# Graph attention with a residual and layer norm: when the residual of the last 26 tiles is gathered

## The chip, the cores and the metric

The kernel runs on one core of a Trainium2 chip. The metric is the device time of one execution in microseconds (us), median over several executions.

## The reference

For each of 16 graphs of 1024 nodes with 512 features: q, k and v are three projections of `x`; each node attends, in 8 heads of 64, to the nodes that its row of the 0/1 matrix `adj` names (one matrix for all graphs); the result is projected, added to `x`, and normalised.

```python
q, k, v = ((x @ W + b).reshape(B, N, 8, 64) for W, b in ((Wq, bq), (Wk, bk), (Wv, bv)))
scores = einsum('bqhd,bkhd->bhqk', q, k) / sqrt(64) + (1 - adj) * -1e9
out = einsum('bhqk,bkhd->bqhd', softmax(scores), v).reshape(B, N, 512)
x = layernorm(x + out @ Wo + bo)          # over the last axis, eps 1e-5, no affine
```

## The kernel before

`adj` is sparse, and the kernel never forms the dense scores. At the start it ranks the nodes by their number of neighbours, and from then on works on *tiles* of 128 nodes in that order: 8 tiles to a graph, 128 in all, numbered `b * 8 + t`. The list of original rows of tile `t` is the column `asked_row[:, t]`. For each tile, `edges(t)` builds the lists of neighbours (`key_row`, `query_row`).

The attention itself runs in *blocks*. One block takes 128 pairs of a query and one of its neighbours: `gather` fetches 128 rows of k and v together (`kvg`, 512 KB, from the scratch `kv_rows` in device memory) by an indirect DMA, and once per tile the 128 query rows (`qt`, 256 KB, from `q_rows`); VectorE multiplies q and k (`products`, L889) and sums by head (`scores`, L893); ScalarE takes the exponential (L903) and, mostly, weighs v with it (`weigh`, L913); VectorE or TensorE adds the blocks of a tile up. A graph has 35 blocks, the whole run 560.

The projections are the other half ("fronts"): for pairs of node tiles of a *later* graph, `x` is loaded (L548, three buffers), transposed by TensorE (`pxT`), copied out by ScalarE (`xT`, L559), multiplied with the weights (a seven-product scheme, `pair`), and written to `q_rows` (L615, tile `q`, two buffers) and `kv_rows` (L628, tile `kv`, five buffers). The last stage, `finish`, multiplies the attention's result with Wo (`po`), adds the residual (`y`, L790), normalises and scatters the rows out (L816).

The order on every engine is written out by one loop over a step number `n`. It runs from -34; blocks 0 to 559 are due at steps 0 to 559, so steps -34 to -1 are a lead-in with the ranking, the lists and the first graph's projections. In step `n` the loop issues `gather(n + 8)`, `products(n + 4)`, `exponentials(n + 3)`, `weigh(n + 2)` or `(n + 1)`, and then as many matmul units of the fronts as its estimate of the step's length allows. Steps are positions in the engines' instruction lists, not times: each engine goes through its own list in order and waits for others by semaphores alone. Indirect DMAs are issued from GpSimd (POOL), plain ones of this part of the program from SyncE (SP); both lists are in order too.

The residual `y` of a tile is the tile's rows of `x` in the ranked order. For tiles 0 to 101 it is gathered straight from `x` when it is needed (L752, from `load_y`). For the last 26 tiles (`SPILL[0]` = 102 and up) it is put in order ahead of time: `sort_residual(i)` gathers the rows of tile 102 + i into an SBUF tile `y_sorted` (POOL, L752) and, two steps on, SP writes it to a scratch `residual[i]` in device memory (L760). Near the end of the run, `load_y` reads it from there with a plain DMA (L769). `y_sorted` shares the six buffers of tag `y` with the `y` of `load_y`, so the gather of copy i waits for the write of copy i - 6.

Two copies go at the end of each step that `SORTED_AT` names:

```python
SORTED_AT = range(-16, -3)
...
if n in SORTED_AT:
    for i in range(2):
        sort_residual(2 * (n - SORTED_AT[0]) + i)
```

Of the kernel before, what the change touches and what calls it, by code (L numbers as in the profile page):

```python
# [35 lines left out]

SPILL = range(102, 112)

SORTED_AT = range(-16, -3)
AHEAD_LAST = 11  # L40

ROWS = 3
# [118 lines left out]
def kernel(  # L161
# [67 lines left out]
    with ExitStack() as main:  # L229
# [122 lines left out]
        def later(k, fn):  # L352
            plan.setdefault(now[0] + k, []).append(fn)
# [397 lines left out]
        def gather_x(y, b, t):  # L751
            nc.gpsimd.indirect_dma_start(  # L752
                out=y, out_offset=None, in_=x_rows,
                in_offset=bass.IndirectOffsetOnAxis(ap=asked_row[:, t:t + 1], axis=0), element_offset=b * N * D,
            )

        def sort_residual(i):
            y = work.tile([P, D], F32, tag="y", name=f"y_sorted_{i}", bufs=Y_BUFS)
            gather_x(y, *divmod(SPILL[0] + i, NT))
            later(2, lambda: nc.sync.dma_start(residual[i], y))  # L760
# [117 lines left out]
        def products(n):  # L878
            b, t, i = blocks[n]
            if t == 0 and i == 0:  # L880
                norms = small.tile([P, NPAIR], F32, tag="lone", name=f"lone_{b}", bufs=1)
                later_last(0, lambda q=QT[b, t]: squares(f"q_{b}", q, norms, lone))
                later(2, lambda: nc.vector.tensor_reduce(lone_norm[:, b:b + 1], norms, axis=AX.X, op=OP.max))
            if i < OWN[t]:
                q = QT[b, t] if i < OWN[t] - 1 else QT.pop((b, t))
            else:
                q = QG.pop(n)
            QK[n] = work.tile([P, D], F32, tag="qk", name=f"qk_{n}", bufs=2)
            nc.vector.tensor_tensor(QK[n], q, KG[n][:, 0:D], op=OP.mult)  # L889

        def scores(n):
            S[n] = small.tile([P, HEADS], F32, tag="s", name=f"s_{n}", bufs=4)
            nc.vector.tensor_reduce(S[n], QK.pop(n).rearrange("p (h d) -> p h d", d=HD), axis=AX.X, op=OP.add)  # L893

        def exponentials(n):

            b, t, i = blocks[n]
            if i == 0:
                PV[n] = work.tile([P, D + HEADS], F32, tag="pv0", name=f"pv_{n}", bufs=3)
            else:  # L900
                PV[n] = work.tile([P, D + HEADS], F32, tag="pv", name=f"pv_{n}", bufs=PV_BUFS)
            bias = absent[:, own[t] + i:own[t] + i + 1] if i < OWN[t] else 0.0
            nc.scalar.activation(PV[n][:, D:], S.pop(n), AF.Exp, bias=bias)  # L903

        def by_act(n):
            b, t, i = blocks[n]
            return 0 < i < OWN[t] or n % 2 == 0 or n < NB // 2

        def weigh(n):
            v, pv = KG.pop(n), PV[n]  # L910
            if by_act(n):
                for h in range(HEADS):
                    nc.scalar.activation(  # L913
                        pv[:, ts(h, HD)], v[:, ds(D + h * HD, HD)], AF.Copy, scale=pv[:, D + h:D + h + 1]
                    )
                return
            nc.vector.tensor_tensor(
                pv[:, 0:D].rearrange("p (h d) -> p h d", d=HD),
                v[:, D:].rearrange("p (h d) -> p h d", d=HD),
                pv[:, D:, None].to_broadcast([P, HEADS, HD]), op=OP.mult,  # L920
            )

        def add_own(n):
            b, t, i = blocks[n]
            pv = PV.pop(n)
            if i == 0:
                PV[b, t] = pv
            else:
                nc.vector.tensor_tensor(PV[b, t], PV[b, t], pv, op=OP.add)  # L929
# [120 lines left out]
        with tc.manual_schedule():  # L1050
# [12 lines left out]
            n = -LEAD_IN  # L1063
            while n < total or plan or rest or urgent or done or finishing or spilled or not guarded:
                now[0] = n
                if n < 0:
                    share = LISTS_SHARE if n > -16 else LEAD_SHARE if n > -LEAD_IN else TRANSPOSE * 1.5
                elif n >= SPILL[0] // NT * NB + NB:

                    share = sum(u[0] for u in fronts) / max(fronts_end - n, 1) + NS * SUM / NB if fronts else LAST_SHARE  # L1070
                elif n % NB == 0:

                    left = sum(u[0] for u in fronts)
                    ahead = EARLY + FIRST * (1 - max(0, n // NB - 1) / (SPILL[0] // NT))
                    goal = fronts_time - (n // NB + 2 + ahead / NB) * batch_time
                    share = (max(0.0, left - goal) + NT * NPAIR * PRODUCT + NS * SUM) / NB
                if 0 <= n + 3 < total:
                    exponentials(n + 3)
                if 0 <= n + 4 < total:
                    products(n + 4)  # L1080
                while gathered[0] < min(n + (AHEAD if fronts else AHEAD_LAST) + 1, total) and blocks[gathered[0]][0] in set_up:
                    gather(gathered[0])
                    gathered[0] += 1
                if 0 <= n + 1 < total and not by_act(n + 1):
                    weigh(n + 1)
                if 0 <= n < total and blocks[n][2] < OWN[blocks[n][1]]:
                    add_own(n)
                if 0 <= n + 4 < total:
                    scores(n + 4)
                if 1 <= n <= total and (n == total or blocks[n][2] == 0):  # L1090
                    normalise(*blocks[n - 1][:2])
                for fn in plan.pop(n, ()):
                    fn()
                if 0 <= n + 2 < total and by_act(n + 2):
                    weigh(n + 2)
                for fn in rest.pop(n, ()):
                    fn()
                credit += share
                if 0 <= n < total and blocks[n][2] >= OWN[blocks[n][1]]:
                    add_up(n)  # L1100
                    credit -= SUM
                for tile_done in done[:0 if fronts and len(done) < LAZY else 1 if fronts else 2] + coming:
                    if tile_done not in loaded and sum(b * NT + t not in SPILL for b, t in Y) < 5:
                        load_y(*tile_done)
                coming[:] = [t for t in coming if t not in loaded]
                if spilled and not fronts and n > last_reload + 2 and sum(b * NT + t in SPILL for b, t in Y) < 3:
                    reload(*spilled.pop(0), reloads)
                    reloads, last_reload = reloads + 1, n
                first_unit = True
                while credit > 0 or urgent:  # L1110
                    if urgent and not (first_unit and fronts):
                        urgent.pop(0)()
                        continue
                    if (
                        not finishing and len(done) > (LAZY if fronts else 0) and n > loaded.get(done[0], n) + 1
                        and n > last_finish + 1 and not total - 2 <= n < total
                    ):
                        finishing = finish(*done.pop(0))
                        last_finish = n
                    units = finishing or fronts  # L1120
                    if not units:
                        if urgent:
                            urgent.pop(0)()
                            continue
                        break
                    cost, fn, ready = units[0]
                    if ready and not ready():
                        if urgent:
                            urgent.pop(0)()
                            continue  # L1130
                        break
                    del units[0]
                    fn()
                    credit -= cost
                    first_unit = False
                credit = min(credit, share)
                preps += prep.pop(n, [])
                preps = [g for g in preps if next(g, True) is None]
                if n in SORTED_AT:
                    for i in range(2):  # L1140
                        sort_residual(2 * (n - SORTED_AT[0]) + i)
                n += 1

    word = nc.values_load(  # L1144
# [32 lines left out]
```

## Time and profile before

| | us |
|---|---|
| median of four executions | 1985.45 (1982.45 to 1996.21) |
| the profiled execution | 1986.11 |
| its span, first to last instruction | 1984.3 |
| TensorE (PE) busy in it | 1913.2 |
| VectorE (DVE) busy | 1780.9 |
| ScalarE (ACT) busy | 1566.8 |
| GpSimd (POOL) busy | 1294.3 |
| the 26 gathers of `y_sorted` are issued | from 75.3 to 145.0 |
| the 26 writes to `residual` are issued | from 80.3 to 151.8 |
| the 26 reads from `residual` are issued | from 1782.1 to 1950.7 |

All times in the trace count from the start of the span. "DMA share" in the tables by stretch is the mean busy share of the core's 16 DMA engines, and can come out a little over 1. A wait is written `waiting instruction <- what ended the wait`, with the total in us, the times it occurred and the longest; `issue` means that nothing the trace shows was waited for, `remote` that what ended it is not among the recorded instructions. Names such as SPq are the queue of instructions of an engine that issues DMAs.

### The profile page before, as it was taken

To read this page: it belongs to the slowest core of one execution; us is meant where nothing else is said; L and a number is where in the kernel's file an instruction comes from. 1 tells how busy PE (TensorE), PEld (TensorE's weight loads), DVE (VectorE), ACT (ScalarE), POOL (GpSimd) and SP (SyncE) were. 2 spreads that over 40 slices of the span, in tenths; PEclk is the share of its full clock that TensorE was granted. 3 is DMA by queue.
4 is the path that set the end of the run, shared out by engine and by line. 5 is a ranking of instruction groups with operands and counts; after the bars stand their busy time and mean duration, and the time that the engine had idled before them with its cause. 6 is when DMAs were issued, how large, how long until landed. Compare 5 with 4: busy or idle time off the path is not lost. (4 is left out here: it accounts for less than half of the span.)

```text
span 1984.3 us, 25833 instructions
## 1 busy us (share of the span) xinstructions
PE 1913.2 (96%) x5379; PEld 923.5 (47%) x5379; DVE 1780.9 (90%) x3745; ACT 1566.8 (79%) x6152; POOL 1294.3 (65%) x1224
## 2 busy tenths in 40 slices
PE   8988999999999999999999999999999999999896
PEld 4434454444545454454545445444444545444443
DVE  3789999989999999999998999999899999999785
ACT  4526878878797888879887887879888798988795
POOL 1563566756777675767667586766757676566784
PEclk9999999999999999999999999999999999999898
DMA  6797887978989788888889788888978889988984
GB/s 255 227 341 247 262 303 248 300 270 278 314 267 318 258 304 282 300 286 281 305 262 321 255 302 274 299 304 266 314 256 285 287 299 322 316 307 287 319 286 146
DMA packets 191140, 563.10 MB, mean 284 GB/s; under 512 B 31711, under 2 KB 31739, under 8 KB 190974
## 3 DMA queue, kind: packets, MB, share of 16 engines
q0 software_dynamic: 121632, 403.22, 62.2%
q1 hardware_dynamic: 66736, 153.16, 20.8%
q10 hardware_dynamic: 2606, 4.99, 0.7%
q14 instruction: 122, 1.00, 0.2%
q8 instruction: 44, 0.72, 0.1%
HBM read 442.25 MB, written 143.71 MB: 295 GB/s over the span
## 5 line engine op out<-in xcount | busy, mean ns | idle before, releaser
L868 POOL DMA_INDIRECT kvg<-kv_rows,key_row x560 | 632.1, 1129 | 434.2 <-ACT pv L903 114.0
L913 ACT ACTIVATE pv<-kvg,pv 128x64 f32<-128x64 f32 x3608 | 908.7, 339 | 0.1
L584 PE MATMUL pq<-wq,xT 128*128 128x512 f32 x1024 | 478.7, 597 | 3.9 <-issue 1.7
L584 PE MATMUL po<-wo,oT 128*128 128x512 f32 x944 | 437.0, 595 | 4.7 <-DVE y L790 1.9
L893 DVE TENSOR_REDUCE s<-qk 128x8 f32<-128x512 f32 x560 | 380.5, 680 | 6.1
L889 DVE TENSOR_TENSOR qk<-qt,kvg 128x512 f32<-128x512 f32 x464 | 317.0, 683 | 3.8 <-DMA kvg<-kv_rows,key_row 3.3
L584 PEld LDWEIGHTS pq<-wq,xT 128*128 128x128 f32 x1024 | 191.3, 191 | 222.8 <-issue 207.3
L584 PEld LDWEIGHTS po<-wo,oT 128*128 128x128 f32 x944 | 175.5, 191 | 206.0 <-issue 191.2
L698 PE MATMUL pp<-t,s 128*128 128x512 f32 x504 | 238.6, 596 | 9.4 <-DVE s L570 9.4
L698 PE MATMUL x<-b,xT 128*128 128x512 f32 x504 | 237.1, 593 | 0.0
L929 DVE TENSOR_TENSOR pv<-pv,pv 128x520 f32<-128x520 f32 x336 | 232.9, 693 | 0.0
L903 ACT ACTIVATE pv<-s,absent 128x8 f32<-128x8 f32 x464 | 135.8, 294 | 106.4 <-DVE s L893 65.9
L816 POOL DMA_INDIRECT out_dram<-y,asked_row x128 | 151.4, 1183 | 38.9 <-issue 26.3
L852 POOL DMA_INDIRECT qt<-q_rows,asked_row x128 | 139.8, 1092 | 36.7 <-issue 34.3
L594 ACT ACTIVATE sq_k<-kv 128x128 f32<-128x128 f32 x512 | 150.7, 300 | 9.7 <-DVE kv L721 8.7
L698 PEld LDWEIGHTS pp<-t,s 128*128 128x128 f32 x504 | 95.2, 191 | 119.1 <-issue 107.1
L698 PEld LDWEIGHTS x<-b,xT 128*128 128x128 f32 x504 | 94.7, 190 | 112.2 <-issue 108.8
L752 POOL DMA_INDIRECT y<-in_x_dram,asked_row x102 | 115.4, 1131 | 30.6 <-issue 29.8
L862 POOL DMA_INDIRECT qg<-q_rows,query_row x96 | 105.7, 1102 | 26.8 <-issue 25.1
L698 PE MATMUL z<-b,s 128*128 128x512 f32 x252 | 118.6, 593 | 1.4 <-issue 0.7
L698 PE MATMUL z<-t,s 128*128 128x512 f32 x252 | 118.6, 593 | 0.0
L698 PE MATMUL pp<-t,xT 128*128 128x512 f32 x252 | 118.4, 592 | 0.0
(193 smaller groups left out, 2614.3 us busy)
## 6 DMA issues: line engine op xcount, KB each, us to landing
kv_rows<-kv SPq DMA_DIRECT2D x128, 512.0 KB
x<-in_x_dram SPq DMA_DIRECT2D x128, 256.0 KB
q_rows<-q SPq DMA_DIRECT2D x128, 256.0 KB
kvg<-kv_rows,key_row POOLq DMA_INDIRECT x560
residual<-y_sorted SPq DMA_DIRECT2D x26, 256.0 KB
y<-residual SPq DMA_DIRECT2D x26, 256.0 KB
adj<-in_adj_dram POOLq DMA_DIRECT2D x8, 512.0 KB
spill<-oT SPq DMA_DIRECT2D x10, 256.0 KB
```

Of the source, the lines that this page charges most:

```text
L584: nc.tensor.matmul(p, lhs()[:, ts(c, P)], w[:, c, :], start=(c == 0), stop=(c == NPAIR - 1))
L594: nc.scalar.activation(sq, s[:, ts(h, P)], AF.Square, scale=scale, accum_out=sums[:, h:h + 1])
L698: nc.tensor.matmul(R[bank], l[:, ts(c, P)], right[:, c, :], start=(first and c == 0), stop=(c == 1), skip_group_check=True,)
L752: nc.gpsimd.indirect_dma_start(out=y, out_offset=None, in_=x_rows, in_offset=bass.IndirectOffsetOnAxis(ap=asked_row[:, t:t + 1], axis=0), ...
L816: nc.gpsimd.indirect_dma_start(out=out_rows[b, t], out_offset=bass.IndirectOffsetOnAxis(ap=asked_row[:, t:t + 1], axis=0), in_=y, in_offse ...
L852: nc.gpsimd.indirect_dma_start(out=QT[b, t], out_offset=None, in_=q_rows[b % ROWS], in_offset=bass.IndirectOffsetOnAxis(ap=asked_row[:, t: ...
L868: nc.gpsimd.indirect_dma_start(out=KG[n], out_offset=None, in_=kv_rows[b % ROWS], in_offset=bass.IndirectOffsetOnAxis(ap=key_row[:, g:g + ...
L889: nc.vector.tensor_tensor(QK[n], q, KG[n][:, 0:D], op=OP.mult)
L893: nc.vector.tensor_reduce(S[n], QK.pop(n).rearrange("p (h d) -> p h d", d=HD), axis=AX.X, op=OP.add)
L903: nc.scalar.activation(PV[n][:, D:], S.pop(n), AF.Exp, bias=bias)
L913: nc.scalar.activation(pv[:, ts(h, HD)], v[:, ds(D + h * HD, HD)], AF.Copy, scale=pv[:, D + h:D + h + 1])
L929: nc.vector.tensor_tensor(PV[b, t], PV[b, t], pv, op=OP.add)
```

## The change

The same 26 copies are made, in the same order, two to a step, in 13 steps as before. The first eight copies stay at steps -16 to -13. The other 18 move from steps -12 to -4 to steps -3 to 5. As the steps are no longer consecutive, the copy's number comes from the position in the list.

```diff
-SORTED_AT = range(-16, -3)
+SORTED_AT = (*range(-16, -12), *range(-3, 6))
...
                 if n in SORTED_AT:
                     for i in range(2):
-                        sort_residual(2 * (n - SORTED_AT[0]) + i)
+                        sort_residual(2 * SORTED_AT.index(n) + i)
```

On PE, DVE and ACT the instructions and their order are the same in both programs. On POOL the 18 gathers move behind the gathers of blocks 0 to 5, and stand two by two between those of blocks 5 to 14; the gather of the first `y` (graph 0, tile 0) follows them. On SP the 18 writes move among the later writes of `q` and `kv` and loads of `x`. The list of block gathers and residual copies on POOL, from the fifth neighbour list on (`codes` is a gather of `adj` rows in `edges`; `s8` stands for `y_sorted` number 8):

```
before: s8 s9 codes4 s10 .. s15 codes5 s16 s17 qt0 kvg0 qt1 kvg1 codes6 s18 s19 kvg2 s20 s21 qt2 kvg3
        s22 s23 kvg4 s24 s25 qt3 kvg5 kvg6 kvg7 qt4 kvg8 kvg9 kvg10 kvg11 qt5 kvg12 kvg13 kvg14 y0 kvg15
after:  codes4 codes5 qt0 kvg0 qt1 kvg1 codes6 kvg2 qt2 kvg3 kvg4 qt3 kvg5 s8 s9 kvg6 s10 s11 kvg7 s12 s13
        qt4 kvg8 s14 s15 kvg9 s16 s17 kvg10 s18 s19 kvg11 s20 s21 qt5 kvg12 s22 s23 kvg13 s24 s25 kvg14 y0 kvg15
```

## The prediction

> **What bounds the kernel now.** I read the shares of the engines first, then the busy time by stretches, then the waits and the order of time where the 18 copies leave and where they arrive. (The page's chain that ended last reaches back only 4 us from the end, so it says nothing here.)
>
> ```profile
> PE 1913.2 (96%) x5379; PEld 923.5 (47%) x5379; DVE 1780.9 (90%) x3745; ACT 1566.8 (79%) x6152; POOL 1294.3 (65%) x1224
> ```
>
> TensorE is busy for 96% of the span. What a change wins in the lead-in is kept only if it lets PE start its long, nearly full stretch earlier. In the next answer the columns are the length, the busy time of PE, weight loads, DVE, ACT and POOL, the granted clock, the DMA share and GB/s.
>
> ```profile
> 75.00:100.00 25.00, 25.00 (x65) 11.46 (x64) 19.66 (x56) 7.04 (x25) 13.99 (x14) 1.00 0.90 305
> 100.00:125.00 25.00, 19.71 (x50) 7.87 (x48) 23.65 (x69) 5.36 (x21) 11.75 (x12) 1.00 0.91 310
> 125.00:150.00 25.00, 21.23 (x57) 9.65 (x57) 18.01 (x47) 6.53 (x29) 19.30 (x19) 1.00 1.01 373
> 150.00:175.00 25.00, 18.27 (x56) 9.01 (x55) 23.32 (x57) 10.67 (x43) 4.80 (x5) 0.93 0.67 246
> 175.00:200.00 25.00, 24.86 (x77) 11.93 (x76) 24.31 (x57) 20.98 (x88) 9.31 (x10) 1.00 0.77 246
> ```
>
> Until 100 us PE is full. From 100 to 175 it is idle for 5.29 + 3.77 + 6.73 = 15.8 us while DVE is busy 23.65, 18.01 and 23.32 of each 25: the neighbour lists are DVE work, and this stretch is DVE's. It is also where the DMA engines are full, 0.91 and 1.01. From 175 on PE is full again. So the prize is at most those 15.8 us, and only the part that the DMA traffic causes. In the stretch 138 to 160:
>
> ```profile
> DVE kv L726 <- ACT sq_q L594: 5.5, 1, 5.5
> ...
> PE pp L698 <- DVE s L570: 4.0, 1, 4.0
> ...
> DVE est L491 <- remote: 1.4, 1, 1.4
> ```
>
> DVE loses 5.5 + 1.4 = 6.9 us. The program's list of waits says what L726 (writing `kv`) needs: TensorE's `z`, recorded as done at 142.7, ScalarE's squares of the tile that had the buffer, done at 134.2, and the write of that tile to `kv_rows`, which SP issued at 132.8. DVE went on at 148.7. The `sq_q` that the answer names is not in that list; it only happened to end then. The `kv` write is the one candidate that no record shows done by 143. But a load of `x` on SP that waits for the same write went out at 145.8, so the write can explain DVE's wait to there and not the last 2.9 us. L491 waits for one small matmul recorded at 142.5 and was released at 150.8 by something not recorded. Both fall where DMA is fullest: 411 GB/s at a share of 1.04 from 145 to 150, 412 GB/s from 150 to 155. PE pays afterwards, since `s` on DVE (L570) comes late:
>
> ```profile
> 151.25 1.88 PE L698 MATMUL x<-b,xT 128*128 128x512 f32 x4
> 153.12 1.31 PE L513 MATMUL pe<-kl,of 128*128 128x82 f32 x10
> 158.41 3.40 PE L698 MATMUL pp<-t,s 128*128 128x512 f32 x4 [3.97 <-DVE s L570]
> ...
> 165.51 1.88 PE L698 MATMUL x<-b,xT 128*128 128x512 f32 x4
> ```
>
> Four matmuls of the same form take 1.88 us at 165.5 and 3.40 us at 158.4, after the gap of 3.97 us.
>
> **What the Trainium skill says.** (1) "DMA: Bandwidth & Descriptors", section "Issuing engines are not separate DMA queues": transfers started from any engine run on the same 16 DMA engines and interleave. The trace agrees: between 146 and 150 POOL's queue takes 58.5% of them and SP's 45.3%. (2) The same page, "Anatomy of one DMA": DMA engines don't wait on semaphores, the issuing sequencer does. So a copy that waits for its buffer holds up all behind it on POOL; the trace has 2.1 us of it, at 117.6 below. (3) "TensorE: Matmul & The Clock Gate", Part 1: after an idle window of about 3.4 us the array runs at half clock. The granted clock is 0.79 from 155 to 160 and 1.00 before, which agrees.
>
> **The change, part by part.**
> *Size.* A copy reads 256 KB and writes 256 KB; 18 of them are 18 x 0.524 = 9.4 MB. At the 410 GB/s of the fullest stretch that is 23.0 us of all DMA engines.
>
> *Taken away, steps -12 to -4.* The stretch 100 to 150 moved 17.1 MB; without the copies (part of whose traffic runs on to 158) it is about half full. DVE's own work there stays: 94% busy from 95 to 142, so nothing is won before 142. After that, on DVE 6.9 us go; on PE the waits of 4.0, 0.7 and 0.5 us (the last two shown as "issue" for `z` and `pq` between 143 and 150) and 3.40 - 1.96 = 1.4 us of slow clock, 6.6 us. With both engines alike I take **6 us won**. Bounds: 0, if these stalls have another cause (the "remote" release is unexplained); 9, if the 2.8 us that PE waits at 172 go too. What is late next is DVE, without a gap.
>
> *Moved past on POOL.* 18 gathers with the 0.3 us between two, 1.25 us each: 22.5 us of POOL, 2.5 us ahead of each of the gathers kvg6 to kvg14. POOL stands idle for about 36 us between 151 and 205, mostly for `weigh` of the block whose buffer the gather takes. So issue time is covered. If it weren't, it would be 2.5 us a step.
>
> *Moved into, as bandwidth.* Before, the free DMA share from 155 to 195 in stretches of 5 us is 0.26, 0.23, 0.50, 0.67, 0.27, 0.30, 0.30, 0.25: 2.78 x 5 = 13.9 us. The other 9.1 of 23.0 us must go into 138 to 155, which is half empty once the old copies are gone (17 x 0.5 = 8.5). It fits with nothing to spare. The first six, s8 to s13, can start about 138: kvg1 was issued at 126.8, and seven gathers of 1.3 us lie between.
>
> *The buffers.* A copy takes the `y` buffer of the copy six earlier, once that is written. The two legs under full DMA:
>
> ```profile
> 117.64 0.94 POOL L752 DMA_INDIRECT y_sorted<-in_x_dram,asked_row  x1 [2.10 <-DMA residual<-y_sorted]
> ...
> 144.98 0.95 POOL L752 DMA_INDIRECT y_sorted<-in_x_dram,asked_row  x1 [0.30 <-issue]
> ...
> 160.34 0.98 POOL L868 DMA_INDIRECT kvg<-kv_rows,key_row  x1 [7.98 <-DVE est L482]
> ...
> 190.33 0.99 POOL L868 DMA_INDIRECT kvg<-kv_rows,key_row  x1 [2.28 <-ACT sums L535]
> 191.62 0.96 POOL L752 DMA_INDIRECT y<-in_x_dram,asked_row  x1 [0.30 <-issue]
> ```
>
> Gather 25 was issued at 145.0 and its write went out at 151.8, so a gather took at most 6.9 us. Copy 16, at 117.6, waited for write 10, issued at 108.2: 9.5 us for a write. Six copies can turn round in 16.4 us, 5.5 us for a step of two. The new steps are shorter, 3 to 7 us. Forward with everything 6 us earlier than before: write 8 stands on SP behind the `kv` writes at 160.0, now 154, so s14 can go at 154 + 9.5 = 163.5, s20 at 180, and y0, which takes the buffer of s20, at 196.3. Before it went at 191.6, which would be 185.6 now.
>
> *Who waits for that.*
>
> ```profile
> 187.94 0.68 DVE L889 TENSOR_TENSOR qk<-qt,kvg 128x512 f32<-128x512 f32 x1
> ...
> 205.85 0.68 DVE L889 TENSOR_TENSOR qk<-qt,kvg 128x512 f32<-128x512 f32 x1
> ...
> 207.65 0.68 DVE L790 TENSOR_TENSOR y<-po,y 128x512 f32<-128x512 f32 x1
> ```
>
> The ninth `products` (block 8) is at 187.94 and kvg8 was issued at 160.34: 27.6 us in hand. Block 14 has 205.85 - 190.33 = 15.5, y0 has 207.65 - 191.62 = 16.0. In the new order kvg12 goes behind s20 and s21 at about 182.5 and is used at 193 (199.2 before): 10.7 in hand, above 6.9. y0, issued at 196.3 and landed by 203.2, is used by DVE at 201.6: **1.6 us late**, in the in-order list of DVE. The smaller risk on SP is that `q`, `kv` and `x` transfers stand behind a residual write that waits for its gather; SP lost 18.1 us to that in all before, and two buffers of `q` some 20 us apart cover 5 us of it. I add 0.4 and take **2 us given back**; bounds 0 (the legs are maxima) and the slower case below. DVE gets no instruction more. The reads of `residual` from 1782 us on are as they were.
>
> Sum: 6 - 2 = 4 us less than the profiled 1986.1 us (span 1984.3, to 1980.3). That execution is 0.7 us above the median of 1985.45, which is nothing here; the forecast median is 1981.5 us. About 0.5% (9.9 us) is what a measurement of this kernel can tell from no change, so this counts as the same.
>
> **The rivals.**
> *The stalls are not the copies' doing*: they stay at 142 to 158, or come back at another place of the lead-in because DVE is 94% busy there. For it: the "remote" release, PE's own records that say its part was done. Against: nothing like it appears where DMA is less full. About 1985.5, with up to 3 us either way.
>
> *Slower: the turn of the buffers sets the pace.* The reckoning above has six legs in a row from write 8 to y0's landing. Each us that a leg is longer delays y0 by 6 us, and POOL holds kvg15 and all later gathers behind it. For it: kvg gathers, residual gathers and both kinds of writes share the engines, with no spare share left, and SP holds writes back for gathers. Against: the legs I used are the longest that the trace shows at a share of 1.0. With 3 us more a leg y0 is 1.6 + 18 = 20 us late; less the 6 won that is +14, and about 1997 once the late steps have thinned the traffic. It decides from about 2.5 us a leg: 1.6 + 15 - 6 = 10.6 us, over 0.5%.
>
> *Faster by over 0.5%*: PE gets back 11 of its 15.8 idle us. The 7.8 us of them before 142 lie beside a full DVE, so this needs DVE instructions to get shorter as well. About 1974.
>
> That the change doesn't do what it says is excluded by the lists of POOL and SP: the 18 copies do stand behind kvg5.
>
> **How the numbers follow.** The forecast (won 6, back 0 to 4): 0.52, 1979 to 1984. No effect: 0.26, counted as the same. Slower: 0.17, of which 0.16 beyond 0.5%. Faster: 0.05. That makes faster 0.05, same 0.79, slower 0.16. The range runs from 1975 (9 won, nothing given back, 1 to 2 us of scatter between runs) to 1996; it leaves out about 0.04 below and 0.14 above.
>
> **What would show it.** Right: DMA share about 0.5 from 100 to 138; L726 of that pair without a wait; no 4 us gap of PE before `pp` and no clock of 0.79; the first block's exponential some 6 us earlier; the copies issued from about 138 to 186; y0 issued near 196, and DVE's wait at L790 under 3 us. Wrong: the 5.5 us still there with a half-empty DMA; or DVE waits at L889 or L790 of over 10 us in all between 180 and 215; or PE idle after 175 that was not there.

## The result, and the profile after

| | before | after |
|---|---|---|
| median | 1985.75 us (1981.11 to 1996.21, 63 executions) | 1990.88 us (1985.41 to 1997.48, 42 executions) |
| the profiled execution, and its span | 1986.11, 1984.3 | 1990.22, 1988.4 |

The ratio after to before is 1.0019, 95% interval 1.0011 to 1.0027: **slower by 3.8 us, where 4 us less was forecast**. It is within the 0.5% that was counted as the same and within the range, but on the other side of zero. (The means of the two lists, 1990.71 and 1986.92 us, are 3.8 us apart, the medians 5.1.)

The shares of the engines, on the page of the kernel after:

```profile
PE 1916.0 (96%) x5379; PEld 925.0 (47%) x5379; DVE 1781.7 (90%) x3745; ACT 1567.2 (79%) x6152; POOL 1294.2 (65%) x1224
```

The same work, busy for as long. Next the same stretches of the kernel after as in the prediction (length, busy time of PE, weight loads, DVE, ACT and POOL, clock, DMA share, GB/s):

```profile
100.00:125.00 25.00, 19.65 (x50) 7.87 (x48) 23.64 (x69) 5.37 (x21) 4.90 (x6) 1.00 0.47 159
125.00:150.00 25.00, 17.31 (x45) 8.17 (x46) 17.68 (x47) 3.12 (x12) 17.07 (x17) 0.95 0.93 332
150.00:175.00 25.00, 22.32 (x64) 11.07 (x64) 24.10 (x59) 14.70 (x64) 7.14 (x7) 0.91 0.66 217
175.00:200.00 25.00, 24.85 (x77) 12.16 (x76) 23.32 (x55) 19.89 (x84) 15.20 (x15) 1.00 0.98 357
```

From 100 to 125 the DMA share fell from 0.91 to 0.47, as forecast. From 125 to 150 it is 0.93, hardly less than the 1.01 of before, and there PE lost time: 17.31 us busy against 21.23. From 175 on the share is 0.98 where it was 0.77. Finer stretches, and POOL's own list in order of time, show what filled the second row:

```profile
135.00:140.00 5.00, 5.00 (x13) 2.08 (x13) 4.63 (x17) 0.00 (x0) 3.78 (x5) 1.00 0.99 347
140.00:145.00 5.00, 2.84 (x15) 1.79 (x13) 2.35 (x3) 0.59 (x1) 3.78 (x5) 1.00 0.99 394
145.00:150.00 5.00, 2.08 (x3) 1.04 (x4) 1.19 (x2) 0.68 (x2) 1.64 (x2) 0.75 0.87 345
150.00:155.00 5.00, 5.00 (x11) 2.15 (x11) 4.76 (x15) 3.30 (x18) 0.00 (x0) 0.91 0.37 110
```

```profile
134.25 0.99 POOL L868 DMA_INDIRECT kvg<-kv_rows,key_row  x1 [0.30 <-issue]
135.54 0.97 POOL L752 DMA_INDIRECT y_sorted<-in_x_dram,asked_row  x1 [0.30 <-issue]
...
144.75 0.94 POOL L752 DMA_INDIRECT y_sorted<-in_x_dram,asked_row  x1 [0.30 <-issue]
146.00 0.95 POOL L852 DMA_INDIRECT qt<-q_rows,asked_row  x1 [0.30 <-issue]
161.03 1.00 POOL L868 DMA_INDIRECT kvg<-kv_rows,key_row  x1 [14.08 <-ACT pv L913]
163.46 0.95 POOL L752 DMA_INDIRECT y_sorted<-in_x_dram,asked_row  x1 [1.42 <-DMA residual<-y_sorted]
...
197.63 1.20 POOL L752 DMA_INDIRECT y<-in_x_dram,asked_row  x1 [1.66 <-DVE g L717]
```

The first six moved copies, s8 to s13, stand behind `kvg5` and are written in the loop at steps -3 to -1, yet they went out from 135.54 to 144.75. POOL does not wait for the step. It had nothing to wait for until kvg8, whose buffer another block held (14.08 us). So the six gathers fell into the very stretch in which the kernel before lost time, and the DMA is at 0.99 there until 145. The waits of the stretch 138 to 160, and PE in order of time:

```profile
ACT xT L559 <- remote: 7.2, 1, 7.2
...
PE pq L584 <- DVE g L717: 5.1, 1, 5.1
DVE g L717 <- issue: 4.3, 1, 4.3
...
DVE kv L726 <- remote: 1.6, 1, 1.6
```

```profile
142.56 0.28 PE L489 MATMUL poff<-est,before 128*128 128x1 f32 x2
147.92 5.15 PE L584 MATMUL pq<-wq,xT 128*128 128x512 f32 x8 [5.09 <-DVE g L717]
152.91 1.88 PE L698 MATMUL pp<-t,xT 128*128 128x512 f32 x4
```

The stall is still there under other names: DVE waits 4.3 us at L717 where it waited 5.5 at L726, PE waits 5.1 us ahead of `pq` and runs its eight matmuls in 5.15 us. At the other end, DVE in order of time:

```profile
196.73 0.69 DVE L717 TENSOR_TENSOR g<-pp,w 128x512 f32<-128x512 f32 x1 [1.03 <-PE pxT L555]
...
208.17 0.68 DVE L790 TENSOR_TENSOR y<-po,y 128x512 f32<-128x512 f32 x1
```

y0 was issued at 197.63 (196.3 was forecast) and DVE does not wait at L790: the first `y` came in time. DVE's 1.03 us at L717 is all that this trace loses in the new place.

To follow gains through the run I read the start of each block's sum by head (`s<-qk` on DVE, L893) and take the difference to the profiled execution of before, where block 1 is at 156.66 us. In the kernel after, block 1 is at -0.75 us, block 11 at +0.51, block 480 at +0.83 and block 559 at +4.0. So 5.2 of the 6 us to be won are missing at once, 1.1 more go at block 11, and the 3 us at the end come in stretches where both programs have the same order of instructions.

### The profile page after: what moved, and what is told of

Read it like the earlier page. It is cut to its first block, busy times and chain, and to the rows that moved or that the text cites. A ratio compares the mean times of both kernels' runs of the same rounds, so it can differ in the third digit from the quotient of the medians.

```text
span 1988.4 us, 25835 instructions
## 1 busy us (share of the span) xinstructions
PE 1916.0 (96%) x5379; PEld 925.0 (47%) x5379; DVE 1781.7 (90%) x3745; ACT 1567.2 (79%) x6152; POOL 1294.2 (65%) x1224
## 3 DMA queue, kind: packets, MB, share of 16 engines
q1 hardware_dynamic: 66736, 153.16, 20.8%
## 5 line engine op out<-in xcount | busy, mean ns | idle before, releaser
L893 DVE TENSOR_REDUCE s<-qk 128x8 f32<-128x512 f32 x560 | 380.4, 679 | 6.7 <-DVE qk L889 0.6
L889 DVE TENSOR_TENSOR qk<-qt,kvg 128x512 f32<-128x512 f32 x464 | 317.1, 683 | 3.7 <-DMA kvg<-kv_rows,key_row 2.2
L752 POOL DMA_INDIRECT y<-in_x_dram,asked_row x102 | 116.6, 1143 | 32.0 <-issue 29.1
```

Source lines behind the costliest of these rows:

```text
L752: nc.gpsimd.indirect_dma_start(out=y, out_offset=None, in_=x_rows, in_offset=bass.IndirectOffsetOnAxis(ap=asked_row[:, t:t + 1], axis=0), ...
```

## The experiments

Each was timed against the kernel before on the same chip, with one chip to a batch; chips and loads differ by up to 17 us in the median of before, so only the ratios and runs of one batch are set beside each other. "Block 1" is the difference to the first trace of before, as above. In some kernels the edit shifts the line numbers a little.

| batch | kernel | median | median of before | ratio, 95% interval | block 1 |
|---|---|---|---|---|---|
| 1 | before_again | 1995.43 | 1995.86 | 1.0007 (0.9989 to 1.0025) | +0.2 |
| 1 | after_again | 1996.96 | 1995.86 | 1.0006 (0.9991 to 1.0021) | -0.5 |
| 1 | take_away | 1998.25 | 1995.86 | 1.0016 (1.0004 to 1.0029) | -5.1 |
| 1 | add_alone | 1994.75 | 1995.86 | 1.0001 (0.9987 to 1.0016) | -0.9 |
| 2 | from_step_0 | 1985.08 | 1980.05 | 1.0024 (1.0015 to 1.0034) | -5.2 |
| 2 | six_only | 1984.80 | 1980.05 | 1.0027 (1.0016 to 1.0038) | -3.7 |
| 2 | one_a_step | 1982.56 | 1980.05 | 1.0014 (1.0005 to 1.0023) | -5.1 |
| 2 | half_width | 1979.66 | 1980.05 | 0.9998 (0.9988 to 1.0008) | -6.8 |
| 3 | left_out | 1990.46 | 1994.11 | 0.9980 (0.9966 to 0.9994) | -7.1 |
| 3 | before_third | 1993.68 | 1994.11 | 0.9990 (0.9972 to 1.0008) | +3.9 |
| 3 | after_third | 1995.81 | 1994.11 | 1.0011 (0.9995 to 1.0027) | +1.6 |
| 3 | take_away_again | 1995.70 | 1994.11 | 1.0014 (1.0001 to 1.0028) | -7.3 |
| 4 | direct_18 | 1990.90 | 1979.19 | 1.0056 (1.0042 to 1.0070) | -4.9 |
| 4 | direct_26 | 1998.19 | 1979.19 | 1.0096 (1.0080 to 1.0113) | -6.7 |
| 4 | left_out_again | 1978.50 | 1979.19 | 0.9989 (0.9979 to 0.9998) | -4.7 |
| 4 | before_fourth | 1978.43 | 1979.19 | 0.9998 (0.9988 to 1.0007) | -6.3 |

Up to 2.1 us of a difference at block 1 is older than any copy: DVE's write of `bo_bc` (L346, at 74.12 us in the first trace of before, where the first copy is issued at 75.28) stands at -0.3 to +2.1 us in the others. Less this start, block 1 is at -6.7 to -7.0 in the nine traces without full-size copies at 135 to 150, at -5.7 in six_only, at -6.8 in before_fourth, and from -1.3 to +2.6 in the other seven.

My theory was that of the prediction, amended by the trace: full DMA makes the stall, and the first six moved copies kept it alive. The rivals were that the stall has another cause, and that the new place costs what is lost.

**Batch 1: the two halves of the change apart.** *before_again* and *after_again* are the two kernels once more.

> The kernel before, unchanged, as its own control: ratio to the kernel before 1.000 +- 0.001 under every theory. Its second trace shows what moves between two executions of one program. If the +3 us that the changed kernel's trace showed after 1780 us (and the +0.6 around block 103) is chance of one execution, this trace differs from the first one by as much there, while its block times up to 250 us agree within 0.3 us.

> The changed kernel, unchanged: +3.7 us (ratio 1.002) again. Theory N (the new place costs it in the lead-in): its second trace has block 20 about 0.5 us or more behind the kernel before, and clocks under 1.00 around 145 to 155 and 170 to 175 us again. Theory L (the loss is made late in the run): block 20 within 0.5 us, and the bulk of the loss after 1780 us again.

*take_away* empties the old place and leaves the new one empty as well:

```diff
-SORTED_AT = range(-16, -3)
+SORTED_AT = {n: (2 * (n + 16), 2 * (n + 16) + 1) for n in range(-16, -12)}
+SORTED_AT |= {64 + 16 * i: (8 + i,) for i in range(18)}
...
+                for i in SORTED_AT.get(n, ()):
+                    sort_residual(i)
```

> The taking away alone: copies 0 to 7 where they were, the 18 others one at a time, one every 16 steps from step 64 to 336, so neither at steps -12 to -4 nor at -3 to 5. Theory N: the old place costs some us and the new one more, so this is faster than the kernel before, by up to 6 us (ratio 0.997). Rival S (the stall at 138 to 150 us is not the copies' doing, the old place costs nothing): no change, 1.000, and DVE still idle for 5 to 7 us between 142 and 151 us. If single copies far from the lead-in cost anything there, a loss of 1 to 3 us whatever the lead-in does; the block times at 250 us tell that apart.

*add_alone* keeps all 26 copies and makes the 18 a second time, at steps -3 to 5, into scratch that nothing reads:

```diff
...
+                if n in range(-3, 6):
+                    for i in range(2):
+                        sort_residual(8 + 2 * (n + 3) + i, again=True)
```

> The adding alone: all 26 copies where they were, and the 18 once more at steps -3 to 5 into a scratch of their own. Theory N: slower by 3 to 8 us than the kernel before (ratio 1.002 to 1.004), made before 250 us. Theory L or chance: within 1 us.

The stretches of take_away:

```profile
125.00:150.00 25.00, 22.64 (x60) 10.27 (x59) 23.52 (x68) 6.31 (x29) 12.14 (x13) 1.00 0.85 298
150.00:175.00 25.00, 22.34 (x67) 11.20 (x66) 24.10 (x59) 15.79 (x67) 5.22 (x5) 0.93 0.46 151
```

No stall: DVE is busy for 23.52 us from 125 to 150 (18.01 before), and block 1 comes 5.1 us early, 6.8 less the start. That is the prediction's step "taken away", and its size. Yet the timed median is 0.16% slower. So the gain of the lead-in does not arrive, or something takes it back. In after_again the trace repeats the stall (block 1 at -0.5) and has a second one in the new place, 6.1 us, in a stretch with the DMA share at 1.00:

```profile
204.24 0.69 DVE L726 TENSOR_TENSOR kv<-z,g 128x512 f32<-128x512 f32 x1 [6.06 <-remote]
```

```profile
195.00:205.00 10.00, 9.42 (x22) 3.71 (x20) 3.94 (x8) 6.67 (x29) 7.85 (x8) 1.00 1.00 367
```

add_alone has the first stall in its trace and loses some 4.5 us more in the new place (block 10 at +0.4, block 14 at +5.0), and yet its ratio is 1.0001, at most 1.0016: a second set of copies costs nothing that the timing shows. I have no reason for that.

**Batch 2: which copies keep the stall.** *from_step_0* moves all 18 to steps 0 to 8, behind kvg8 and its long wait; *one_a_step* puts one in each of steps 0 to 17.

```diff
-SORTED_AT = range(-16, -3)
+SORTED_AT = (*range(-16, -12), *range(0, 9))
...
+SORTED_AT |= {i: (8 + i,) for i in range(18)}
```

(The first added line is from_step_0; the last is one_a_step, written as in take_away.)

> The 18 copies at steps 0 to 8 in place of -3 to 5: the first of them then stands on POOL behind the gather of block 8, which waits for block 0's buffer (155 to 160 us), and can't be issued earlier. Theory R (POOL runs ahead of the steps; copies 8 to 13 were issued at 135 to 146 us and kept the stall at 142 to 150 alive): block 1 about 5 us earlier than in the kernel before (at 151.5 in place of 156.7, as in the taking away alone), DVE without the 5 us wait there. The fullness of DMA then moves to 160 to 215 us, so a wait of 1 to 6 us on DVE after block 10; block 20 between -4 and +1. Rival S (those copies have no part in the stall): block 1 at -0.7 again.

> The 18 copies at steps 0 to 17, one to a step. Theory R and that it is the fullness of DMA which costs: block 1 at -5, and with half as many copies to a step no more than 1 to 2 us lost up to block 30: block 32 at about -4, the time 0.998 of the kernel before. Rival Y (copies among the first blocks cost by their place in the lists of POOL and SP and by the shared y buffers, not by their bytes): as much lost as with two to a step, 2 to 6 us by block 32, no gain.

*six_only* moves only s8 to s13, to steps -3 to -1, and the other twelve one by one from step 64. *half_width* does all 18 from step 64, and puts stand-ins of half the bytes (half a row each, into scratch) where the kernel after has the copies.

```diff
...
+SORTED_AT |= {n: (2 * (n + 7), 2 * (n + 7) + 1) for n in range(-3, 0)}
+SORTED_AT |= {64 + 16 * i: (14 + i,) for i in range(12)}
...
+                if n in range(-3, 6):
+                    for i in range(2):
+                        half_copy(8 + 2 * (n + 3) + i)
```

(The first two lines are six_only, the last three half_width.)

> Copies 8 to 13 at steps -3 to -1 as in the change; 14 to 25 one at a time from step 64 on. Theory R: the stall at 142 to 150 is there, block 1 at about -0.7, nothing more is lost after it, so block 20 at about -0.5. Rival: if the stall needs more traffic than six copies bring, block 1 at about -5.

> The real copies 8 to 25 one at a time from step 64 on; at steps -3 to 5, where the change has them, 18 stand-ins with the same instructions, waits and buffers but half the bytes (128 rows of 1 KB, into a scratch that nothing reads). If bytes decide: the stall at 142 to 150 shrinks by half or goes, block 1 between -5 and -2.5, and no wait of DVE over 1 us from block 5 to 20. If the places in the lists and buffers decide: block 1 at -0.7 and the same waits as the change.

Less the start, block 1 is at -6.8 in from_step_0, one_a_step and half_width, and at -5.7 in six_only, where DVE waits 1.30 us for `z` after a stretch at a clock of 0.81 (135 to 140). I took this batch for a test of whether the bytes under way at 135 to 150 make the stall. It is none: not one of its four traces has the stall, there is no trace of before from its chip, and batch 4 has a trace of before that stands at -6.8 as well, with all copies in their old place. What the batch does show lies later. From block 1 to 32 from_step_0 loses 4.8 us and one_a_step 4.6, while half_width loses 0.2 and six_only nothing. Most of it in from_step_0 is 7 us at block 17 to 18, of which some comes back. The second `y` of the run, on POOL and then on DVE, in order of time:

```profile
206.03 0.94 POOL L752 DMA_INDIRECT y_sorted<-in_x_dram,asked_row  x1 [0.51 <-issue]
...
210.53 1.19 POOL L752 DMA_INDIRECT y<-in_x_dram,asked_row  x1 [0.30 <-issue]
```

```profile
218.43 0.69 DVE L790 TENSOR_TENSOR y<-po,y 128x512 f32<-128x512 f32 x1 [7.52 <-DMA y<-in_x_dram,asked_row]
```

This `y` stands behind the last copies on POOL, goes out at 210.53, and DVE waits for it until 218.43. That is the slower rival's waiting instruction, L790, one tile later, in a kernel in which the copies come later than in the kernel after; but POOL waits for no buffer just there, the gather is only late in the list and takes up to 7.9 us to land. (The first `y` waits 2.59 us for the write of a residual, goes out at 192.44 and is in time.) The timed ratios of from_step_0, six_only and one_a_step are again 0.14 to 0.27% slower, though their traces are ahead of the first trace of before by 3.7 to 5.2 us at block 1. For six_only the trace shows no loss up to block 32 that would explain it.

**Batch 3: the price of the copies.** *left_out* drops copies 8 to 25, and tiles 110 to 127 read one of the first eight instead, so that the later reads keep their number and size (their own residual is left out).

```diff
-SORTED_AT = range(-16, -3)
+SORTED_AT = range(-16, -12)
...
-                nc.sync.dma_start(Y[b, t], residual[b * NT + t - SPILL[0]])
+                nc.sync.dma_start(Y[b, t], residual[(b * NT + t - SPILL[0]) % 8])
```

> Copies 8 to 25 are left out altogether; tiles 110 to 127 take the residual of one of the first eight copies instead, so the number and size of the reads from 1782 us on stay the same. This prices the copies themselves and tells whether the lead-in's 5 to 7 us reach the end. Theory (the copies' traffic causes the stall at 142 to 150 in every execution, and what the lead-in wins is kept): block 1 starts about 5 us earlier in the trace, and the timed median is 4 to 7 us lower, ratio 0.9965 to 0.998. Rival (the timed executions do not have the stall, or the full TensorE stretch later gives the time back): block 1 again about 5 us earlier in the trace, ratio 1.000 +- 0.0013. Second rival (moved copies cost time wherever they lie, and take_away was slower by its late copies alone): ratio under 0.998 here, and take_away_again 3 us or more above this run.

> Copies 0 to 7 as before, 8 to 25 one at a time every 16 steps from step 64. Theory (late single copies cost something each): 3 us or more above left_out, ratio 1.0005 to 1.0025. Rival (single copies behind a full TensorE are free): the same as left_out within 1.5 us. In both, block 1 starts about 5 us earlier than in the kernel before.

> The kernel before once more, for a trace and a repeat ratio on this chip. All theories: ratio 1.000 within its interval; DVE waits 4 to 7 us at L717 or L726 between 140 and 152, and PE pays a slow pq or pp. If the stall is absent in this trace, it is not in every execution, and the lead-in part of the forecast is wrong as a mean.

> The changed kernel once more. Theory (its first six moved copies keep the stall alive, and the new place makes a second one at 196 to 220 in some executions): ratio 1.001 to 1.003, block 1 within 1 us of the kernel before, block 16 from 0.5 to 6 us late. Rival (the 1.0019 was scatter between loads of a program): ratio within 0.999 to 1.001.

On one chip and in one batch, the 18 copies cost 1994.11 - 1990.46 = 3.7 us in the old place, 1995.81 - 1990.46 = 5.4 in the new one, and 1995.70 - 1990.46 = 5.2 spread singly over steps 64 to 336. By the ratios the first has an interval of about 3 us to either side and the others of about 4, so the places are not told apart here. take_away_again and left_out run alike to block 1 (-7.3 and -7.1) and part after that: at block 340 they stand at +3.7 and -0.9, and from block 345 to 347 take_away_again loses 7.5 us more. In order of time on DVE, 20 us after the last copy was issued at 1278.32:

```profile
1292.87 0.68 DVE L718 TENSOR_TENSOR g<-pp,w 128x512 f32<-128x512 f32 x1
1298.89 0.69 DVE L727 TENSOR_TENSOR kv<-z,g 128x512 f32<-128x512 f32 x1 [5.33 <-remote]
```

take_away lost 5.3 us at the same place, left_out has no wait of DVE there. But left_out has such waits elsewhere, with no copy anywhere near: 3.96 us at L614 (1204.40) and 4.67 us at L717 (1316.50). So that the last copy makes the wait at 1298.89 is not shown. The DMA share is 0.92 from 1290 to 1295: the middle of the run has hardly more room than the lead-in. (On the page of before the two large queues alone take 62.2% and 20.8% of the DMA engines' time over the whole span.)

**Batch 4: no copy at all.** In *direct_18* tiles 110 to 127 gather their residual straight from `x` when they need it; in *direct_26* all tiles do, and no copy is made.

```diff
-SORTED_AT = range(-16, -3)
+SORTED_AT = range(-16, -12)
...
-            if b * NT + t >= SPILL[0]:
+            if SPILL[0] <= b * NT + t < SPILL[0] + 8:
```

(direct_18; direct_26 has `SORTED_AT = ()` and `if False:`.)

> Copies 8 to 25 are not made at all; tiles 110 to 127 gather their residual straight from x when they need it, as tiles 0 to 101 do, so 18 x 0.5 MB of DMA less in the lead-in, 18 plain reads less on SP and 18 gathers more on POOL from 1800 us on. Theory (the copies' traffic costs time at every place, 3 to 7 us, by what left_out showed): block 1 is 5 to 7 us early, and the median is 2 to 7 us lower, ratio 0.9965 to 0.999. Rival (the end is POOL's: it is busy for 80% there, and 18 gathers of 1.25 us delay the last blocks' gathers): 5 to 20 us more than left_out, ratio 1.001 to 1.008, with DVE waiting at L889 for kvg after 1800.

> None of the 26 copies is made; all tiles gather the residual straight from x. Theory: as direct_18, with DMA emptier from 75 to 100 us too, but TensorE is full there, so no more than 1 us better: ratio 0.996 to 0.999. Rival (POOL at the end decides): another 8 gathers, 10 us of POOL, so slower than direct_18 by 2 to 8 us.

> As left_out (copies 8 to 25 left out, tiles 110 to 127 take the residual of one of the first eight copies) on another chip. Theory: ratio 0.9965 to 0.999 again. Rival (the 0.9980 was scatter between loads): 0.9995 to 1.001.

> The kernel before once more, for its own lead-in on this chip and the repeat ratio: 1.000 within its interval, and DVE waits of 4 to 7 us at L717 or L726 between 140 and 152.

By its number the rival was right: 0.56% and 0.96% slower, from 5 and 4 executions. At block 440 both are 5.5 to 8.8 us ahead of the first trace of before (before_fourth, on their own chip, is 9.3 ahead), and after block 520 they lose 11 and 22 us. From 1850 to 1950, first direct_26, then before_fourth (same columns as above):

```profile
1850.00:1900.00 50.00, 37.22 (x99) 17.47 (x97) 33.81 (x91) 33.95 (x119) 40.19 (x46) 0.90 0.74 237
1900.00:1950.00 50.00, 37.15 (x82) 17.07 (x83) 33.95 (x84) 41.71 (x151) 40.95 (x41) 0.83 0.79 259
```

```profile
1850.00:1900.00 50.00, 41.14 (x112) 19.77 (x111) 41.85 (x110) 42.90 (x154) 41.50 (x45) 0.90 0.81 273
1900.00:1950.00 50.00, 45.63 (x117) 22.35 (x116) 41.15 (x106) 47.21 (x168) 38.74 (x41) 0.93 0.77 262
```

POOL is hardly busier than before (40.2 and 41.0 of 50, against 41.5 and 38.7), but PE has 37.2 and 37.2 us in place of 41.1 and 45.6. In the waits from 1780 on, it is not L889 that waits, as the rival had it; DVE and TensorE wait longer for the normalisation's small steps on POOL and for what follows them; direct_26 first, then before_fourth.

```profile
DVE stats L809 <- POOL stats L806: 28.2, 15, 4.0
...
PE poT L966 <- DVE o L958: 17.0, 4, 8.1
```

```profile
DVE stats L809 <- POOL stats L806: 10.4, 10, 2.8
...
PE poT L966 <- DVE o L958: 7.2, 4, 2.7
```

In direct_26 POOL goes from one instruction to the next with 0.31 us between them or less from 1880 to 1897, and the steps at L806 stand in that list behind the added gathers (L752). So what the reads from `residual` spare the end is worth more than the copies cost in the lead-in; that it is spared through POOL's list is argued from these waits. left_out_again repeats the price only weakly: 0.11% (0.02 to 0.21%) by its ratio, while its median is 0.7 us under that of before and level with that of before_fourth.

The surprise is before_fourth. Its lead-in, in stretches of 5 us, and DVE's `kv` in it:

```profile
140.00:145.00 5.00, 4.54 (x19) 2.65 (x18) 4.73 (x12) 3.87 (x19) 4.09 (x4) 1.00 1.02 387
145.00:150.00 5.00, 5.00 (x13) 2.15 (x12) 4.79 (x11) 0.10 (x1) 3.78 (x5) 1.00 1.03 402
150.00:155.00 5.00, 5.00 (x21) 2.85 (x20) 4.86 (x13) 2.59 (x10) 2.76 (x3) 1.00 1.03 390
155.00:160.00 5.00, 5.00 (x16) 2.40 (x15) 4.86 (x9) 3.29 (x18) 0.98 (x1) 1.00 1.04 411
```

```profile
143.09 0.68 DVE L717 TENSOR_TENSOR g<-pp,w 128x512 f32<-128x512 f32 x1
143.97 0.69 DVE L726 TENSOR_TENSOR kv<-z,g 128x512 f32<-128x512 f32 x1 [0.20 <-DVE g L717]
```

**No stall, with the DMA share at 1.02 to 1.04**, as full as in the first trace. DVE waits 0.20 us at L726 where it waited 5.5, and block 1 is at -6.3, like the kernels whose old place is empty.

What sets before_fourth apart from the stalled traces is in another record. A trace also keeps the times at which semaphores rose. In the eight traces of batches 2 and 4 the semaphore that TensorE raises has 1041 rises, and each of the 1039 instructions of TensorE that raise it has a rise within 0.06 us of its recorded end. In the ten other traces, of the first comparison and of batches 1 and 3, only 791 to 821 rises are recorded, and some come late, in the stalls up to 6.9 us after the nearest recorded end. So there are two kinds of trace, and they go by batch. Among the ten with late rises, all 7 with full-size copies at 135 to 150 stall, and none of the 3 without. Among the eight with prompt rises none stalls, with the copies in the old place (before_fourth) or without. The medians of before go the same way: 1985.75, 1995.86 and 1994.11 us in the first kind, 1980.05 and 1979.19 in the second. Whether the chip or the recording makes the two kinds, no run here tells.

## Why the prediction was right or wrong

1. *DVE and PE stall at 142 to 158 and it is the copies' traffic: right for one kind of trace, but the wait was read wrongly.* Among the traces with late TensorE rises, those with full-size copies all through 135 to 150 (three of before, three of after, add_alone) all show the stall, and those without (take_away twice, left_out) do not. The eight of batches 2 and 4 say nothing on this, since none of them stalls. before_fourth shows that a full DMA is not enough, and there the first rival ("not the copies' doing") fits. I had the `kv` write as the one candidate for L726. It was not: SP's own wait for that write's semaphore took 0.02 us at 143.63, and L726 went on 0.08 us after TensorE's semaphore rose at 148.61. The load of `x` at 145.8 and L491 at 150.8 follow such rises too (145.75, 150.76).

2. *6 us won: right in size where the stall is, nothing where it is not.* Less the start, block 1 of the three traces with late rises and an empty place is at -6.9 us on average, against +0.9 for the three stalled traces of before: 7.8 us. In batch 4 it is at -6.7 to -6.8 with the place empty and at -6.8 in before_fourth: 0. By its two ratios left_out keeps 4.0 us in batch 3 and 2.2 in batch 4. I priced the stall of one execution as if every execution had it. (In the sum of 6.6 us for TensorE the slow clock is 1.5 us by the lines shown, 3.40 - 1.88, not 1.4.)

3. **The step that failed: "the other 9.1 of 23.0 us must go into 138 to 155, which is half empty once the old copies are gone ... It fits with nothing to spare."** By its own figures 9.1 us were to go into 8.5. The start was right (about 138 was forecast, 135.54 came), but this refills the stretch whose emptiness was to bring the 6 us. The sum counted the same room twice: once as the cause of the win, once as the place for the copies. The share of 125 to 150 was 0.93, not about 0.5, and 0.7 of the 6 us were won in that trace; less the start, block 1 is at -0.4 to -0.7 in all three traces of after, where -6 was forecast. take_away and left_out, on the chips of after_again and after_third, show the other side: there the place stays empty, and the stall is gone. The prediction's own test named this, but "with a half-empty DMA": the DMA was not.

4. *2 us given back through the turn of the `y` buffers: the times came out by luck, and the mechanism was not the one.* y0 was issued 1.3 us later than reckoned, but two errors cancel in this. Write 8 went out at 159.70 and not at 154, since the 6 us were not won; and s14 went 3.8 us after it, not 9.5. POOL waited 8.4 us in all for residual writes. Nobody waited for y0, since DVE came to it at 208.17 and not at the 201.6 of the forecast. What the new place cost is another stall at a DMA share of 1.00 to 1.04: 1.1 us in the first trace, 6.1 in after_again, 2.8 in after_third (block 8 to 18, in small pieces), a mean of 3.3; the two stalled traces of before on those chips lose 0.7 there. The slower rival did not happen in the kernel after. In from_step_0 DVE did wait for a `y`, 7.5 us for the second, though mostly because its gather stood late in the list.

5. *The sum.* With the medians of batch 3: what the old place costs is paid again in the new one (3.7 against 5.4 us), which gives +1.7; the first comparison gave +3.8. In batches 1 and 3 the interval of after includes no change, so that it is slower is shown by the first comparison alone. All of this fits a change that moves a cost and at most adds a little to it. Not shown: why add_alone, with both places full, is not slower; why take_away, with neither stall in its lead-in, is not faster; why the timed gain of left_out is less than the trace's; and what makes the two kinds of trace. The kernel after was never traced where the rises are prompt. Batch 2, which has prompt rises, is slower than before in spite of early blocks; if before on that chip runs like before_fourth, this follows for from_step_0 and one_a_step, but no trace of before from that chip shows it.

## What to carry to other kernels

A step in an instruction list is not a time: before moving work to a later step on a queue that seldom waits, look up when that queue reaches the place, and check that the stretch to be relieved is not the one that is filled. A stall seen in one execution is a sample: look at the same stretch in traces of other executions and other chips before pricing its removal, and set a variant beside a trace of the unchanged kernel from its own chip. When a wait has several candidates, look up which semaphore rose just before it ended; a full DMA next to a wait is not yet its cause. In this kernel the two large queues keep the DMA engines busy for 83% of the run, and no place for the copies came out clearly cheaper than the old one; a variant that leaves them out tells the most that a move can bring.

## What the runs showed of the hardware

In the stalls of the first trace of after, DVE (4.3 us), ACT (7.2 us) and SP (9.0 us at the load of `x`) all wait for TensorE work that the records show as done at 140 to 143, and go on at 147 to 149. I had expected a wait for a DMA. The view of waits names no releaser ("remote" or "issue"), but the record of semaphores does for two of them: ACT and SP go on 0.02 us after a rise of TensorE's semaphore at 149.30, with three more rises within 0.16 us of it. So it is TensorE's signal that came late, or the matmuls themselves, whose ends are modelled in a trace. No run here shows what held it.

The gap has a price of its own. After gaps of 5.09, 6.73 and 5.94 us (after, after_again, after_third) the eight matmuls of `pq` took 5.15, 6.20 and 5.13 us, against 3.70 without one in the first trace of before, and the granted clock was 0.75 from 145 to 150. The Trainium skill, "TensorE: Matmul & The Clock Gate", Part 1, says that an idle window slows the array; the traces agree, with 1.4 to 2.5 us for each gap.

The same program had a median of 1985.75, 1995.86 and 1994.11 us in the batches whose traces have late rises and of 1980.05 and 1979.19 in the two with prompt ones. That the two differences go together is seen in these five batches; that the late rises cause the longer times is not shown.
